# A fourth seven-product slot in the first batch, the tokens' transposes in three calls, and a new hand-made order

## The chip, the cores and the metric

The kernel runs on one core of one Trainium2 chip. The metric is the device time of one execution in microseconds (us); lower is better. Times of the kernel before are given as the median of three runs, with the lowest and the highest.

## The reference

The reference is a gated feed-forward block with a norm ahead of it, for x of 4 batches of 1024 tokens with 512 features, and 2048 hidden features:

```python
scale = cond @ norm_w.T + 1.0
ms = jnp.mean(x * x, axis=-1, keepdims=True)
h = x * (scale[:, None, :] * jax.lax.rsqrt(ms + EPS))
u = h @ up_w.T                       # 512 -> 2 x 2048
val, gate = jnp.split(u, 2, axis=-1)
h = val * jax.nn.gelu(gate, approximate=False)
hq = act_quant(h)                    # 8 bits, one scale per token
wq = weight_quant(down_w)            # -1, 0, 1 times one scale
y = hq @ wq.T                        # 2048 -> 512
return y + x
```

## The kernel before

**Tiling.** The tokens go batch by batch. The hidden features are cut into NJ = 16 blocks of 128, and the kernel counts "slots" g = 0 to 63: block j of batch b. The up-projection is made in fp16 with a high and a low part of both operands, in matmuls of 128x128 by 512 tokens. There are two ways to make one block:

- *plain* (`plain`, line 712; the steps `gate`, `gelu`, `value`, `out`): for each half of the tokens 12 matmuls for the gate and 12 for the value, so 48 for a block. ACT makes the gelu from the gate's bank (L758), DVE the product of value and gelu (L768).
- *seven products* (`product`, line 697; the class `Slot`, whose steps are numbered as `slot.g.n`): Strassen's scheme in Winograd's form, seven products of 6 matmuls, so 42 for a block. The products share the banks A, B and E, each starting from what another left there; ACT copies banks between (L804 `first_copy`, L812 `fourth_copy`, L819 `fifth_copy`), makes two gelus (L826, L843), and DVE makes two sums and two products (L832, L840, L849, L852). It needs the sums of quarters of the weights (`s_sum`, then `s_high`, `s_low` for the fp16 parts, L436, L453, L457), which are also written to DRAM for the later batches (`s_spill`, L469). A block that is made by a slot in the first batch gets these sums transposed at once (`s_turn`, L475), two DMAs for a block.

Batches 1 to 3 are made by slots throughout. In the first batch blocks below FAST = NJ - 3 = 13 are plain, and 13, 14 and 15 are made by slots.

**What else the first batch does.** It loads and scales all up-projection weights (`w_load`, `w_range` on ACT in two halves at L322, `w_factor`, `w_scale`), loads the down-projection weights twice: once for their mean (`d_load`, L515, and `d_sum`) and once for rounding (`d_fetch`, L546, then `d_round` on ACT, L550). It also prepares the second batch's tokens in four groups a = 0 to 3 of 256 tokens: `t_load`, `t_square`, `t_root`, `t_scale`, `t_sum`, then `t_high` (ACT, L665) and `t_low` (DVE, L669) write the fp16 parts into a tile `nx`, and `t_turn` (SP, L672) transposes it with a DMA into R. `t_high` and `t_low` come in three parts: the first 2 of 7 quarters, the third, the last 4. The tile `nx` comes from a pool with a single buffer under its tag, so that group a + 1 can be written only when the transpose of group a is done:

```python
self.nx = wpool.tile(
    [P, C_ALL, 2, HALF], F16, name=f"nx_{self.b}_{self.a}", tag="nx", bufs=1
)
```

`d_load.2` and `d_load.3` overwrite places in R which squares of the first tokens (`first_sum`, ACT, L1128) use as scratch. `d_fetch.0` and `d_fetch.1` take places of the tokens' other tiles.

**The order.** Outside the first batch a planner with costs and due times places the side work. The first batch's order is written out: the string FIRST_BATCH is a list of steps, and `take` issues them one after the other. Each engine works off its own queue in this order and waits at the head of it; a step far down the list runs early if its engine is free and its data are there, and late if a step ahead of it on the same engine waits. All DMAs are issued by SP, in the order of the list.

```python
def take(steps):
    for step in steps.split():
        name, *at = step.split(".")
        STEPS[name](*map(int, at))
```

The steps of a slot are, from 0 on: first, first_copy, fourth, fourth_copy, fifth, fifth_copy, second, second_gelu, third, third_out, gate, gate_sum, gate_gelu, value, value_sum, value_out. Of them PE does 0, 2, 4, 6, 8, 10 and 13.

Of the kernel before, what the change touches and what calls it, by code (L numbers as in the profile page):

```python
# [36 lines left out]
C_ALL = 7  # L37
# [14 lines left out]
def glu_quant_kernel(  # L52
# [10 lines left out]
    PE, ACT, DVE, POOL, SP = nc.tensor, nc.scalar, nc.vector, nc.gpsimd, nc.sync  # L63
# [7 lines left out]
    NJ = FF // P  # L71
# [71 lines left out]
    FAST = NJ - 3  # L143
# [434 lines left out]
    class Tokens:  # L578
# [92 lines left out]
        def turn(self):  # L671
            SP.dma_start_transpose(  # L672
                t_view(self.b)[:, self.a].rearrange("p c l k t -> p (c l k) t"),
                self.nx.rearrange("p c l d -> p (c l d)"),
            )
# [627 lines left out]
    def t0_order(n):  # L1303
# [39 lines left out]
        "t_low": lambda a, n: toks[a].low(DVE, n), "t_turn": lambda a: toks[a].turn(),  # L1343
# [13 lines left out]
    def take(steps):  # L1357
# [8 lines left out]
        x_low.0 d_sum.4 x_low.2 o_whole.1.0.1 x_low.3 gate.0.1 w_scale.2.0 out.1.0 w_scale.2.1 w_factor.3  # L1366
        rows_high.2 s_sum.0.2 value.0.1 s_high.0.0 rows_low.2 rows_turn.2 d_sum.5 s_low.0.0 c_largest
        gelu.0.1 gate.1.1 w_scale.3.0 s_sum.1.0.1 t_square.0.0 s_sum.0.3.1 w_load.9 o_WHOLE.3.2.1 s_high.0.1
        w_scale.3.1 s_sum.1.1.1 rows_high.3 value.1.1 s_low.0.1.1 s_spill.0.0 s_sum.1.2.1 s_sum.1.3.1
        s_high.1.0 d_load.0 rows_low.3 w_load.10 gelu.1.1 rows_turn.3 w_range.4 out.1.1 gate.2.0 out.0.1  # L1370
        d_sum.6 w_factor.4 w_range.5 o_sum.0 value.2.0 w_scale.4.0 o_sum.1 w_scale.4.1 w_factor.5 s_high.1.1
        s_low.1.1 w_scale.5.1 c_over gate.2.1 w_gain.2 w_scale.5.0 c_range rows_high.4 s_low.1.0.1
        s_spill.1.0 s_sum.2.1 gelu.2.0 o_sum.2 rows_high.5 value.2.1 d_load.1 gelu.2.1 o_high.1 s_sum.2.0.1
        out.2.0 d_sum.7 rows_low.4 rows_turn.4 gate.3.0 o_high.3 s_sum.2.2.1 s_sum.2.3.1 d_sum.2 out.2.1
        rows_low.5 value.3.0 w_gain.4 gelu.3.0 o_high.2 o_low.1 w_load.6 s_high.2.0 o_low.3 gate.3.1
        s_spill.2.1 s_high.2.1 d_sum.3 w_load.7 s_low.2.1.1 o_sum.3 w_load.11 d_sum.0 rows_turn.5 o_low.2
        w_range.6 value.3.1 s_low.2.0.1 s_sum.3.0 d_sum.1 w_factor.6 s_sum.3.1 c_spread w_scale.6.0 c_rows
        max.0.0.0 gate.4.0 s_spill.4.1 w_scale.6.1 s_spill.3.1 out.3.0 s_spill.2.2 rows_high.6 s_spill.2.0
        max.1.0.0 o_high.0 value.4.0 s_sum.3.2.1 gelu.3.1 o_low.0 w_range.7 rows_low.6 rows_turn.6 gate.4.1
        s_high.3.0 s_sum.3.3.1 out.3.1 t_square.0.1 w_factor.7 gelu.4.0 t_root.0 s_low.3.0.1 s_high.3.1  # L1380
        value.4.1 w_load.8 gelu.4.1 s_spill.3.0 w_scale.7.1 s_sum.4.0.1 c_copy t_load.1 d_total w_scale.7.0
        s_low.3.1.1 s_sum.4.1.1 rows_high.7 c_undo out.4.0 gate.5.0 w_range.8 out.4.1 s_sum.4.2.1 rows_low.7
        rows_turn.7 value.5.0 s_high.4.0 s_low.4.0 w_factor.8 max.0.1.0 w_scale.8.0 w_gain.6 gelu.5.0
        c_store out.5.0 s_spill.5.1 d_spread w_scale.8.1 gate.5.1 s_spill.3.2 rows_high.8 c_load max.1.0.1
# [3 lines left out]
        t_scale.0.0 s_spill.8.1 t_scale.0.1 out.5.1 t_high.0.1 t_high.0.0 s_low.5.0.1 w_gain.8 gate.6.1
        w_range.10 t_sum.0.0.1 s_spill.5.0 s_sum.6.0 s_spill.4.2 gelu.6.1 t_low.0.0 s_spill.7.1 s_sum.6.2.1
        s_sum.6.1.1 value.6.1 t_sum.0.2.1 w_factor.10 t_sum.0.3 s_high.6.0 t_sum.0.1.1 w_scale.10.1  # L1390
        s_low.6.0.1 s_sum.7.0 w_scale.10.0 rows_low.9 rows_turn.9 gate.7.0 t_high.0.2 w_gain.10 gelu.6.0
        t_low.0.2 rows_high.10 value.7.0 t_low.0.1 t_square.1.1 t_turn.0 s_sum.6.3.1 out.6.0 t_square.1.0
# [10 lines left out]
        rows_high.12 max.3.1.0 s_sum.10.1 w_load.13 t_low.1.2 t_square.2.1 value.9.1 s_spill.9.2 rows_low.12
        rows_turn.12 s_high.10.1 t_square.2.0 s_low.10.1.1 out.9.0 s_high.10.0 gate.10.0 t_low.1.0 gelu.10.0
        s_low.10.0.1 t_low.1.1 t_turn.1 max.3.1.1 value.10.0 s_sum.11.0.1 s_sum.11.1.1 gelu.9.1 w_range.13
        out.9.1 s_sum.11.2.1 s_sum.11.3 gate.10.1 w_factor.13 w_scale.13.0 t_root.2 w_load.14 t_scale.2.0
        t_load.3 gelu.10.1 t_scale.2.1 value.10.1 t_sum.2.1.1 w_gain.12 t_sum.2.0 out.10.0 s_high.11.0
# [386 lines left out]
    c = slice(HALF, D)  # L1794
# [29 lines left out]
```

## Time and profile before

| | |
|---|---|
| median of 3 runs (lowest, highest) | 721.4 us (721.0 to 722.2) |
| profiled execution, its time | 721.38 us |
| profiled execution, span of the trace | 719.6 us |
| granted TensorE clock over the span | 1.0 |
| share of the span busy: PE, DVE, ACT, POOL | 99%, 82%, 59%, 18% |
| matmuls in the trace | 3670 |
| TensorE's share of the chain that ended last | 99% |
| HBM read and written | 52.71 MB and 23.09 MB |

PE is the matmul engine (TensorE), PEld its weight loads, DVE VectorE, ACT ScalarE, POOL GpSimd, SP the engine that issues the DMAs. "L712" is line 712 of the kernel before. In a row of a group, a name such as `nx<-xt` is the tile that is written and the one that is read; "x51" is the number of instructions; behind the bar stand busy time in us and the mean duration of one in ns; behind the next one the idle time of the engine just before them, and who ended it. In a timeline a row begins with the start and the duration in us, and a bracket gives the engine's idle time before it. SPq is SP's DMA queue: the duration there is that of the issue, and the landing comes later.

### The profile page before, as it was taken

What the parts mean: (1) busy time and instruction counts of PE and PEld (TensorE: products, weight loads), DVE (VectorE), ACT (ScalarE), POOL (GpSimd) and SP (SyncE); (2) the same over time, 40 slices, a digit from 0 to 9 for tenths busy, and PEclk for the clock granted to TensorE, in tenths of its full rate; (3) what the DMA queues carried; (4) which work ended last, traced back from release to release, by engine and by line L of the source; (5) the groups of instructions that cost most, each with busy time, mean ns of one, the idle gap of its engine ahead of it and who ended that gap; (6) DMA issues with size and microseconds to landing.
All of it is one profiled execution on the core that took longest, in us unless ns stands there. A gap on an engine that the chain in (4) does not pass through costs nothing.

```text
span 719.6 us, 10204 instructions
## 1 busy us (share of the span) xinstructions
PE 713.8 (99%) x3670; PEld 360.2 (50%) x3670; DVE 591.3 (82%) x888; ACT 422.2 (59%) x700; POOL 128.9 (18%) x133
## 2 busy tenths in 40 slices
PE   8999999999999999999999999999999999999998
PEld 4544444444444446665444445665444444445854
DVE  8899899888698879897788868876689888755896
ACT  6998875776568774544335676544433665333473
POOL 1611323421100115340100031460020000000120
PEclk9999999999999999999999999999999999999999
DMA  7899878999886656777744646775944544453253
GB/s 277 265 279 288 250 192 240 260 213 234 225 188 120 131 161 147 206 179 169 150 101 118 130 96 195 172 172 160 210 103 103 102 102 102 100 103 94 104 155 138
DMA packets 225204, 121.18 MB, mean 168 GB/s; under 512 B 187113, under 2 KB 196733, under 8 KB 225154
## 3 DMA queue, kind: packets, MB, share of 16 engines
q1 hardware_dynamic: 225002, 120.41, 66.8%
q8 instruction: 28, 0.46, 0.3%
q14 instruction: 22, 0.18, 0.1%
q10 hardware_dynamic: 152, 0.13, 0.1%
HBM read 52.71 MB, written 23.09 MB: 105 GB/s over the span
## 4 chain that ended last, share of the span: by engine, by line
PE 99%; ACT 0%; DVE 0%; issue 0%
PE A L697 37%; PE E L697 18%; PE po L1061 9%; PE B L697 9%; PE pg L712 9%; PE pv L712 9%; PE po_end L1013 4%; PE pz L1178 1%; PE ptx L1162 1%; PE pv L783 0%; PE po_B L1061 0%; PE pg L783 0%; PE pw L382 0%; PE po_E L1061 0%; PE po_A L1061 0%; ACT R L1128 0%
## 5 line engine op out<-in xcount | busy, mean ns | idle before, releaser
L697 PEld LDWEIGHTS <-SXY 128*128 128x128 f16 x2058 | 201.3, 98 | 235.6
L697 PE MATMUL A<-R,SXY 128*128 128x512 f16 x1140 | 263.4, 379 | 0.0
L697 PE MATMUL E<-R,SXY 128*128 128x512 f16 x576 | 140.0, 379 | 0.0
L832 DVE SCALAR_TENSOR_TENSOR H<-A,sg,t 128x512 f32<-128x512 f32 x51 | 38.2, 750 | 71.7 <-PE A L697 71.5
L984 DVE TENSOR_TENSOR H<-H,am 128x1024 f32<-128x1024 f32 x64 | 76.0, 1212 | 0.0
L843 ACT ACTIVATE t<-t,sg 128x512 f32<-128x512 f32 x51 | 36.7, 720 | 63.0 <-DVE t L840 62.8
L697 PE MATMUL B<-R,SXY 128*128 128x512 f16 x294 | 71.5, 379 | 0.0
L903 DVE TENSOR_REDUCE gm<-H 128x512 f32<-128x1024 f32 x56 | 69.0, 1233 | 1.1
L712 PEld LDWEIGHTS <-SXY 128*128 128x128 f16 x390 | 38.0, 98 | 46.0 <-DVE SXY L424 0.4
L826 ACT ACTIVATE t<-B,sg 128x512 f32<-128x512 f32 x51 | 35.1, 687 | 38.5 <-PE B L697 38.3
L919 POOL PARTITION_ALL_REDUCE am<-R x8 | 14.4, 1795 | 231.5 <-DVE R L905 231.5
L1061 PE MATMUL po<-wd,R 128*128 128x256 fp8e4 x416 | 52.4, 273 | 0.0
L819 ACT COPY t<-A 128x512 f32<-128x512 f32 x51 | 29.7, 581 | 35.8 <-PE A L697 35.4
L1061 PEld LDWEIGHTS <-R 128*128 128x128 bf16 (+1 forms) x448 | 43.8, 98 | 8.9
L812 ACT COPY v<-E 128x512 f32<-128x512 f32 x51 | 29.9, 586 | 31.2 <-PE E L697 30.8
L804 ACT COPY B<-A 128x512 f32<-128x512 f32 x51 | 29.2, 572 | 32.1 <-PE A L697 31.5
L712 PE MATMUL pg<-R,SXY 128*128 128x512 f16 x204 | 46.8, 379 | 0.0
L852 DVE SCALAR_TENSOR_TENSOR H<-v,sg,t 128x512 f32<-128x512 f32 x51 | 40.0, 785 | 6.6 <-ACT t L843 6.6
L849 DVE TENSOR_TENSOR v<-A,v 128x512 f32<-128x512 f32 x51 | 34.8, 683 | 10.8 <-PE A L697 8.7
L712 PE MATMUL pv<-R,SXY 128*128 128x512 f16 x186 | 43.4, 379 | 0.0
L992 ACT ACTIVATE H<-H 128x1024 f32<-128x1024 f32 x38 | 39.9, 1050 | 5.2 <-DVE H L984 5.2
L905 DVE TENSOR_TENSOR R<-R,gm 128x512 f32<-128x512 f32 x56 | 40.4, 721 | 1.1
(237 smaller groups left out, 944.1 us busy)
## 6 DMA issues: line engine op xcount, KB each, us to landing
SXY<-s_dram SPq DMA_DIRECT2D x46, 256.0 KB, 3.1
H<-in_L_cond_up_w_dram SPq DMA_DIRECT2D x13, 512.0 KB, 4.4
s_dram<-SXY SPq DMA_DIRECT2D x16, 384.0 KB, 3.2
SXY<-s_dram SPq DMA_DIRECT2D x46, 128.0 KB, 3.3
xr<-in_x_dram SPq DMA_DIRECT2D x19, 256.0 KB, 3.0
out_dram<-xr SPq DMA_DIRECT2D x19, 256.0 KB, 2.6
H<-in_x_dram SPq DMA_DIRECT2D x8, 512.0 KB, 6.6
R<-in_L_cond_down_w_dram SPq DMA_DIRECT2D x8, 512.0 KB, 6.5
```

Source lines behind the costliest of these rows:

```text
L697: PE.matmul(o, s[:, w, k, :], operand(g // NJ, c, l, k), start=start and n == 0, stop=stop and n == len(TERMS) - 1, skip_group_check=True,)
L712: PE.matmul(ps, a[k // 2][:, w, k % 2, :], XP[:, l, k, h * TOK : (h + 1) * TOK], start=n == 0, stop=n == len(terms) - 1,)
L826: ACT.activation(self.t1, self.B, AF.Gelu, scale=gain(self.g, 1))
L832: DVE.scalar_tensor_tensor(h_half(self.g, 0), self.A, gain(self.g, 0), self.t1, ALU.mult, ALU.mult)
L843: ACT.activation(self.t2, self.t2, AF.Gelu, scale=gain(self.g, 1))
L849: DVE.tensor_tensor(self.v, self.A, self.v, ALU.add)
L852: DVE.scalar_tensor_tensor(h_half(self.g, 1), self.v, gain(self.g, 0), self.t2, ALU.mult, ALU.mult)
L903: DVE.tensor_reduce(gm[0], v, AX.X, ALU.max, apply_absolute_value=True)
L905: return [largest, lambda: DVE.tensor_tensor(m, m, gm[0], ALU.max)]
L984: DVE.tensor_tensor(v, v, r.to_broadcast([P, 2, TOK]), ALU.mult)
L992: ACT.activation(v, v, AF.Copy, bias=MAGIC)
L1061: PE.matmul(po, w[:, j], m, start=start and j == 0, stop=stop and j == n - 1, skip_group_check=True,)
```

## The change

Three things are changed. Block 12 of the first batch is made by a slot (FAST goes from NJ - 3 to NJ - 4), so blocks 12 to 15 are. `Tokens.turn` takes a part, and transposes the first 2 quarters, the third, or the last 4 (8, 4 and 16 blocks of 128x128) in a DMA of its own; the list calls it three times for each of the four groups. The list itself is new throughout: 619 steps for 601. Lines behind the split are one further down in the kernel after (L697 is L698 there, L672 is L673). Below, the first lines of the list and its end are shown; the middle, left out, is likewise in another order.

```diff
--- before.py
+++ after.py
@@ -140,7 +140,7 @@
     )
     A21 = R[:, 0, 6144 : 6144 + 768].bitcast(F16).rearrange("p (n w f) -> p n w f", n=3, w=2)
 
-    FAST = NJ - 3
+    FAST = NJ - 4
     T0 = wd.bitcast(F16).rearrange("p a b c d -> p (a b c d)")
     T0 = T0.rearrange("p (c l k t) -> p c l k t", c=4, l=2, k=2)
 
@@ -668,10 +668,11 @@
             for n, f in self.parts()[slice(part, None if part is None else part + 1)]:
                 eng.tensor_tensor(n[:, :, 1], f, n[:, :, 0], ALU.subtract)
 
-        def turn(self):
+        def turn(self, part=None):
+            c = slice(0, C_ALL) if part is None else (slice(0, 2), slice(2, 3), slice(3, 7))[part]
             SP.dma_start_transpose(
-                t_view(self.b)[:, self.a].rearrange("p c l k t -> p (c l k) t"),
-                self.nx.rearrange("p c l d -> p (c l d)"),
+                t_view(self.b)[:, self.a, c].rearrange("p c l k t -> p (c l k) t"),
+                self.nx[:, c].rearrange("p c l d -> p (c l d)"),
             )
 
 
@@ -1340,7 +1341,7 @@
         "t_load": token_load, "t_square": lambda a, h: toks[a].square(h),
         "t_root": lambda a: toks[a].root(), "t_scale": lambda a, h: toks[a].scale(made["sc"], h),
         "t_sum": lambda a, n, e=0: toks[a].sum(n, BOTH[e]), "t_high": lambda a, n: toks[a].high(n),
-        "t_low": lambda a, n: toks[a].low(DVE, n), "t_turn": lambda a: toks[a].turn(),
+        "t_low": lambda a, n: toks[a].low(DVE, n), "t_turn": lambda a, n: toks[a].turn(n),
         "max": lm, "o_whole": lambda m, k, h: t0_whole(m, k, h, POOL),
         "o_WHOLE": t0_whole, "o_sum": t0_order,
         "o_high": lambda c: t0_high(T0_AT[c], c), "o_low": lambda c: t0_low(T0_AT[c], c),
@@ the list FIRST_BATCH: first lines, and from the second group of token transposes on
- w_load.3 d_load.6 d_load.3 d_load.4 d_load.5 t_load.0 d_load.2 s_sum.0.1 o_whole.2.2.0 gate.1.0
- x_scale.6 w_range.3 x_scale.7 gelu.1.0 o_whole.0.0.0 turn.4 w_range.2 turn.5 turn.6 turn.7 w_load.5
- x_high.1 value.1.0 w_factor.2 x_high.0 d_load.7 s_sum.0.0.1 w_load.4 x_low.1 x_high.3 x_high.2
...
- gate.11.1 t_high.2.1 t_low.2.0 t_square.3.1 t_low.2.1 t_square.3.0 s_low.12.0.1 t_turn.2 t_root.3
- w_factor.14 value.11.1 s_sum.12.3.1 gelu.11.1 t_scale.3.0 w_scale.14.0 s_sum.13.0.1 w_scale.14.1
- out.11.1 s_high.12.1 s_low.12.1 gate.12.0 gelu.12.0 w_load.15 s_spill.12.0 s_sum.13.2 out.11.0
- s_sum.13.1.1 value.12.0 s_sum.13.3.1 s_high.13.0 rows_high.14 s_low.13.0.1 s_turn.13.0 s_sum.14.0
- s_high.13.1 t_high.3.0 gate.12.1 s_low.13.1.1 s_sum.14.2 w_range.15 s_spill.13.0 s_turn.13.1
- s_sum.14.1.1 rows_low.14 s_spill.13.2 s_sum.14.3.1 value.12.1 rows_turn.14 w_factor.15 gains
- w_scale.15.1 t_scale.3.1 s_high.14.0 s_low.14.0 t_sum.3.0.1 s_turn.14.0 w_scale.15.0 out.12.0
- slot.13.0 t_sum.3.2.1 s_sum.15.0 slot.13.2 slot.13.1 t_sum.3.1.1 max.4.0.0 s_high.14.1 s_low.14.1
- rows_high.15 slot.13.4 s_spill.14.0 w_gain.14 t_high.3.1 t_sum.3.3.1 slot.13.6 slot.13.5 max.4.0.1
- s_turn.14.1 gelu.12.1 s_sum.15.2.1 out.12.1 s_spill.14.2 slot.13.7 s_high.15.0 slot.13.13 d_fetch.0
- t_high.3.2 s_sum.15.3.1 s_sum.15.1.1 slot.14.0 rows_low.15 rows_turn.15 slot.14.1 t_low.3.0
- slot.14.2 t_low.3.2 slot.13.3 slot.14.6 slot.13.14 s_spill.10.2 d_round.0 s_low.15.0.1 slot.13.8
- t_low.3.1 s_turn.15.0 max.5.0.0 s_high.15.1 s_low.15.1 w_gain.15 slot.14.7 slot.14.4 d_fetch.1
- t_turn.3 max.5.0.1 slot.13.10 slot.14.5 max.4.1.0 slot.14.13 slot.13.9 slot.13.11 slot.15.0
- max.4.1.1 slot.13.12 s_turn.15.1 max.5.1.0 slot.15.1 slot.15.2 slot.14.3 slot.14.14 s_spill.15.0
- s_spill.15.2 slot.15.6 slot.15.7 d_fetch.3 max.5.1.1 slot.13.15 slot.14.8 slot.14.9 slot.15.3
- s_spill.11.2 d_round.1 slot.15.4 d_fetch.2 s_spill.14.1 max.6.0.0 s_spill.15.1 slot.15.5 slot.14.10
- s_spill.13.1 s_spill.12.2 d_sign.0 max.6.0.1 slot.15.13 slot.14.11 d_sign.1 max.6.1.0 slot.14.12
- max.6.1.1 slot.15.14 slot.14.15
+ d_load.2 w_load.3 d_load.6 d_load.4 t_load.0 s_sum.0.1 o_whole.0.0.0 gate.1.0 w_range.3 x_scale.7
+ o_whole.2.2.0 x_scale.6 turn.4 w_range.2 gelu.1.0 turn.5 w_load.4 turn.6 turn.7 d_load.5 value.1.0
+ d_load.3 x_high.2 w_factor.3 s_sum.0.0 d_load.7 x_high.0 c_largest w_factor.2 x_high.1 s_sum.0.2.1
+ x_low.0 x_high.3 s_sum.0.3 s_high.0.0 x_low.1 x_low.2 w_scale.2.0 s_low.0.0 w_scale.3.1 x_low.3
...
+ s_low.13.0.1 s_turn.13.0 s_sum.13.3.1 rows_low.14 slot.12.0 slot.12.1 t_low.2.2 slot.12.2
+ rows_turn.14 max.3.1.0 s_high.13.1 s_low.13.1 s_sum.14.0.1 slot.12.4 slot.12.5 slot.12.3 t_low.2.0
+ s_spill.13.0 w_gain.14 s_sum.14.2 s_turn.13.1 slot.12.6 slot.12.7 out.11.1 s_spill.13.2 slot.12.13
+ t_turn.2.2 s_sum.14.3 w_range.15 slot.13.0 s_sum.14.1.1 t_square.3.1 w_factor.15 slot.13.2 slot.13.1
+ max.3.1.1 t_square.3.0 slot.12.14 s_high.14.0 slot.13.6 t_root.3 t_scale.3.1 w_scale.15.1
+ w_scale.15.0 slot.12.8 s_low.14.0.1 s_turn.14.0 rows_high.15 t_sum.3.0 slot.13.4 rows_low.15
+ s_spill.14.0 s_sum.15.0.1 slot.12.10 t_turn.2.0 slot.13.5 t_scale.3.0 t_sum.3.2 slot.13.7 slot.12.9
+ slot.13.3 slot.13.13 rows_turn.15 slot.12.11 s_high.14.1 t_sum.3.3 s_low.14.1.1 slot.12.12 slot.14.0
+ slot.14.1 slot.13.14 s_turn.14.1 s_sum.15.1.1 slot.14.2 s_sum.15.2.1 t_sum.3.1.1 s_spill.14.2
+ s_high.15.0 s_low.15.0 t_low.2.1 max.4.0.0 t_high.3.2 slot.14.6 t_high.3.0 slot.12.15 s_spill.15.0
+ slot.13.8 s_turn.15.0 t_low.3.2 slot.14.3 w_gain.15 slot.14.4 slot.14.5 d_fetch.0 s_sum.15.3.1
+ t_turn.2.1 t_low.3.0 slot.13.10 slot.13.9 d_fetch.1 s_high.15.1 s_low.15.1 s_turn.15.1 slot.14.13
+ slot.13.11 slot.13.12 max.4.0.1 slot.15.0 slot.14.7 slot.14.14 slot.15.1 max.5.0.0 t_turn.3.0
+ slot.15.2 slot.13.15 slot.15.3 s_spill.11.2 slot.15.6 max.5.0.1 t_turn.3.2 max.4.1.0 slot.14.8
+ slot.15.7 d_round.1 s_spill.13.1 max.4.1.1 slot.15.4 d_fetch.2 gains s_spill.15.2 max.5.1.0
+ d_round.0 s_spill.9.2 slot.14.10 slot.15.5 slot.14.9 d_sign.0 max.5.1.1 slot.15.13 slot.14.11
+ t_high.3.1 slot.14.12 slot.15.14 d_sign.1 t_low.3.1 t_turn.3.1 slot.14.15 max.6.0.0 d_fetch.3
+ max.6.0.1 max.6.1.0 s_spill.15.1 s_spill.10.2 s_spill.14.1 max.6.1.1
```

More of the change, by code (lines that the diff above doesn't have):

```diff
@@ L1368, in glu_quant_kernel @@
[L1368 to L1372, printed above, removed]
@@ L1388, in glu_quant_kernel @@
[L1388 to L1392, printed above, removed]
@@ L1403, in glu_quant_kernel @@
[L1403 to L1407, printed above, removed]
@@ new lines, in glu_quant_kernel @@
+        t_high.1.2 s_low.9.1.1 s_sum.10.3 gate.9.1 out.9.0 s_spill.10.1 t_high.1.0 s_spill.9.0 s_high.10.0
+        w_load.13 t_low.1.2 s_low.10.0.1 value.9.1 t_turn.1.2 s_high.10.1 w_scale.12.0 t_high.1.1
+        s_sum.11.1.1 gelu.9.1 s_sum.11.0 rows_high.12 gate.10.0 t_low.1.0 t_turn.1.0 t_square.2.0
+        rows_low.12 t_square.2.1 out.9.1 w_range.13 rows_turn.12 s_sum.11.2.1 value.10.0 t_low.1.1
+        s_low.10.1.1 gelu.10.0 max.3.0.1 s_high.11.0 t_turn.1.1 s_sum.11.3 s_low.11.0.1 w_load.14 gate.10.1
```

72 lines of the change are left out of this document (42 added, 30 removed).

## The prediction

> **What bounds the kernel now.** I read first the busy shares and the chain that ended last (the page's parts 1 and 4), then the busy time by stretches, then the chain in order of time around the end of the first batch.
>
> ```profile
> PE 713.8 (99%) x3670; PEld 360.2 (50%) x3670; DVE 591.3 (82%) x888; ACT 422.2 (59%) x700; POOL 128.9 (18%) x133
> PE 99%; ACT 0%; DVE 0%; issue 0%
> ```
>
> ```profile
> 0.00:20.00 20.00, 17.30 (x86) 9.49 (x87) 16.17 (x77) 13.51 (x31) 4.40 (x9) 1.00 0.74 259
> 100.00:120.00 20.00, 20.00 (x95) 9.06 (x93) 19.64 (x33) 12.50 (x24) 7.29 (x7) 1.00 0.76 249
> 155.00:690.00 535.00, 535.00 (x2811) 274.82 (x2810) 431.36 (x566) 284.32 (x448) 78.31 (x79) 1.00 0.62 144
> ```
>
> In the second block the columns are the stretch, its length, then the busy time of PE, weight loads, DVE, ACT and POOL, the granted clock, the DMA share and GB/s. TensorE (PE) is the bound, and has no gap: 535.00 us busy of 535.00 after the first batch, 20.00 of 20.00 in its middle. Two things follow. A matmul that goes away is worth its pitch. And there is no slack downstream in which lost time could come back: whatever PE waits is added to the end in full. DVE is nearly as full in the first batch (19.64 of 20), so the order in which the queues are served decides whether anything is late.
>
> ```profile
> 150.55 2.59 PE pv L712 x12
> 153.14 1.29 PE A L697 x6
> ```
>
> A matmul costs 2.59/12 = 0.216 us in the plain block and 1.29/6 = 0.216 in the slot, so only their number matters.
>
> **The saving.** Block 12 goes from 48 matmuls (four groups of 12) to 42 (seven products of 6): 6 x 0.216 = 1.3 us less on PE. That is all that the change can gain. ACT gives up two gelus and gets one slot's copies; of the slots' sums that POOL and DVE share, POOL gets 27 in the new list where it had 18, and in the quoted stretch it is busy 7.29 of 20 and can take them. I cost these at nothing: DVE, the fuller of the two, is eased by them. If that cover were gone, one cast or subtraction late would be 0.6 to 1.2 us by the rows of these below.
>
> **The new wait, which carries the forecast.** The fp16 copy of a group of tokens, nx, has one buffer. Group 3 may be written into it (t_high.3.2, t_high.3.0, on ACT) only when all transposes of group 2 have landed. Before, t_turn.2 stood ahead of t_high.3.0 in the list. Now t_turn.2.1, the smallest part of it, is the 14th step behind t_high.3.2, and on SP behind s_spill.15.0, s_turn.15.0 and d_fetch.0. So ACT stops at t_high.3.2 until a transpose has been issued and has landed. Behind it on ACT's queue are t_high.3.0, slot.14.3, w_gain.15 and slot.14.5. The last is the copy of slot 14's fifth product out of bank A; PE's slot.14.13 (the value product) writes this bank, and all of PE is behind it.
>
> When does PE want it? The trace has slot 14's first product, and slot 15's with ACT's copy of it:
>
> ```profile
> 159.45 1.46 PE L697 MATMUL A<-R 128*128 128x512 f16 x6
> 168.51 1.46 PE L697 MATMUL A<-R,SXY 128*128 128x512 f16 x6
> ```
>
> ```profile
> 170.06 0.57 ACT L804 COPY B<-A 128x512 f32<-128x512 f32 x1 [1.07 <-PE A L697]
> ```
>
> With one product less ahead of it, slot 14 starts at 159.45 - 1.30 = 158.15 (in the trace's clock). slot.14.13 is the seventh product from there in the list (14.0, 14.2, 14.6, 13.8, 14.4, 13.10, 14.13), so it is wanted at 158.15 + 6 x 1.295 = 165.9.
>
> When does t_turn.2.1 land? It starts from slot 14's first copy, slot.14.1: in the trace such a copy starts 170.06 - 168.51 = 1.55 after its product, here 159.7. Then come s_high.15.0 on ACT, s_low.15.0 on POOL, and four issues on SP:
>
> ```profile
> L453 ACT CAST s_rows<-H 128x512 f16<-128x512 f32 x6 | 3.7, 610 | 0.0
> ```
>
> ```profile
> 155.65 1.16 POOL L457 TENSOR_TENSOR s_rows<-H,s_rows 128x512 f16<-128x512 f32 x1 [1.01 <-ACT s_rows L453]
> ```
>
> ```profile
> 138.69 4.29 SPq L672 DMA_TRANSPOSE R<-nx  x1
> 158.13 0.57 SPq L469 DMA_DIRECT2D s_dram<-s_rows  x1
> 158.75 0.43 SPq L546 DMA_DIRECT2D dn<-in_L_cond_down_w_dram  x1
> 163.55 1.24 SPq L475 DMA_TRANSPOSE SXY<-s_rows  x1
> 284.80 1.19 SPq L483 DMA_TRANSPOSE SXY<-s_dram  x1
> ```
>
> Copy done 160.3, s_high to 160.9, s_low to 162.1; s_spill.15.0 (0.57) from 162.2, s_turn.15.0 (1.24) from 162.8, d_fetch.0 (0.43) from 164.1, t_turn.2.1 from about 164.7 (gaps of some 0.05 between issues are in these rows). The trace has no 4-block transpose of nx: the nearest are those of the later batches, the last row above being one of 4 blocks, and the load just ahead of it in the queue.
>
> ```profile
> DMA to landing us min/median/max: 2.7/3.9/5.3
> dn<-in_L_cond_down_w_dram SPq DMA_DIRECT2D x3, 512.0 KB, 4.7
> ```
>
> The first row is for the line of those transposes (4 and 12 blocks), the second for the loads of d_fetch between 155 and 180. Alone, a 4-block one should be near 2.7 to 3.2. But d_fetch.0, issued 0.6 before, needs 4.7, until 164.1 + 4.7 = 168.8, on the same queue. I take the load as the nearer row and put the transpose just behind it: landed at 169.2 (bounds 167.9 and 169.7).
>
> Then ACT works off what stands before PE's need:
>
> ```profile
> L665 ACT CAST nx<-xt 128x1024 f16<-128x1024 f32 x6 | 6.3, 1042 | 0.1
> L360 ACT ACTIVATE sg<-sw,dx 128x4 f32<-128x4 f32 x7 | 2.0, 292 | 0.0
> L819 ACT COPY t<-A 128x512 f32<-128x512 f32 x51 | 29.7, 581 | 35.8 <-PE A L697 35.4
> L812 ACT COPY v<-E 128x512 f32<-128x512 f32 x51 | 29.9, 586 | 31.2 <-PE E L697 30.8
> 147.75 0.62 ACT L665 CAST nx<-xa 128x512 f16<-128x512 f32 x1
> ```
>
> 1.04 + 0.62 + 0.59 + 0.29 + 0.58 = 3.1, or 2.8 since neighbours overlap by about 0.1. PE goes on at 169.2 + 2.9 = 172.1, where 165.9 was wanted: **6.2 us lost** (4.9 with the early landing, 6.9 with the late one). What was late behind it, DVE's t_low.3.2 and the remaining products of slots 13 and 14, moves with PE and adds nothing.
>
> In the old trace t_turn.2 was issued at 138.69 and t_high.3.0 ran at 147.75 without a wait, so this is a wait that did not exist.
>
> **PE's rate after standing still.** Nothing in this trace shows PE after an idle stretch in the middle. The nearest rows are at its start:
>
> ```profile
> 3.66 2.31 PE L1178 MATMUL pz<-H 128*128 128x512 f16 x5
> 9.22 0.59 PE L1178 MATMUL pz<-H 128*128 128x512 f16 x2
> ```
>
> Five matmuls take 2.31 (0.43 to 0.46 each), later two take 0.59 (0.22 from one to the next, the rest being the last one's own length); the granted clock reads 1.00 over both. PE thus began at half rate and was at full rate by 9.2. A stop of 6 us may bring the half rate back. It costs nothing if not; at worst the half of some 6 us, 3.0. I take 1.7, a little over the middle. The Trainium skill, "TensorE: Matmul & The Clock Gate", section "What's actually happening", says that PE drops to half clock after an idle window of about 3.4 us and comes back after about 3.4 us of work; by that rule the loss would be half of 3.4, 1.7 us. The start agrees with its two rates; that an idle stretch in the middle brings it back, no row here shows.
>
> **The start.** The new list begins with d_load.2, then w_load.3; before, w_load.3 came first and d_load.2 six steps later.
>
> ```profile
> 7.97 0.38 SPq L306 DMA_DIRECT2D H<-in_L_cond_up_w_dram  x1
> 8.61 10.73 SPq L515 DMA_DIRECT2D R<-in_L_cond_down_w_dram  x4
> SPq L515 <- ACT R L1128: 8.1, 1, 8.1
> 15.42 0.66 ACT L1128 ACTIVATE R<-H 128x512 f32<-128x512 f32 x1
> R<-in_L_cond_down_w_dram SPq DMA_DIRECT2D x8, 512.0 KB, 6.5
> H<-in_L_cond_up_w_dram SPq DMA_DIRECT2D x13, 512.0 KB, 4.4
> 21.65 0.74 ACT L1155 ACTIVATE H<-H,rs 128x512 f32<-128x512 f32 x1
> 22.26 0.64 ACT L322 ACTIVATE H<-H 128x512 f16<-128x512 f32 x1
> 23.55 1.91 PE L1162 MATMUL ptx<-ident,H 128*128 128x128 f32 x16
> ```
>
> The 8.1 us wait is d_load.3's, for the last of three squares of ACT's (L1128) whose scratch it overwrites; d_load.2 overwrites the scratch of the first of them (15.42 to about 16.1). So w_load.3, issued at 7.97 before, now waits behind d_load.2 until about 16.6, and lands 4.4 to 6.5 later, 21.0 to 23.1, in a stretch where the queue is full: I take 23.0. Its range (w_range.3, twice 0.61) now stands ahead of x_scale.6 on ACT, which then ends at about 23.0 + 1.2 + 0.7 = 25.0. PE's transposes turn.6 need it, the third of four groups of four, at 23.55 + 8 x 0.11 = 24.4. **0.6 us lost** (0 to 1.5).
>
> **Three calls for one.** The 28 blocks took 4.29 us of SP; three calls of 8, 4 and 16 take about 4.1 by the 4- and 8-block rows. Slot 12 adds two transposes of its rows (s_turn.12, 1.24 each), issued while slots 13 to 15 are still being made. Neither is what ends last. At the end d_fetch.3 stands behind t_turn.3.1, and its rounding on ACT ahead of work that slot 17 needs: it comes out within 0.1 us of the need. I add **0.1** (0 to 1.5).
>
> **The sum.** -1.3 + 0.6 + 6.2 + 0.1 + 1.7 = +7.3 on the profiled execution's 721.38 us (span 719.6), which is the median of the runs shown (721.4): **728.7 us**.
>
> **Rivals.**
> - *The stop without a change of rate.* For it: the granted clock is 1.00 in every row quoted. Against: the start's two rates. 721.4 + 5.6 = 727.0; with the early landing and no early stall 721.4 - 1.3 + 4.9 = 725.0.
> - *The saving alone, no slower.* If t_turn.2.1 is out early enough, ACT never stops: the six matmuls go, 720.1, within what counts as the same. It decides at a landing of 165.9 - 2.9 = 163.0 or earlier, that is, an issue by 160 instead of 164.7, so s_low.15.0 and s_spill.15.0 would have to run five microseconds earlier than slot.14.1 lets them. Against it stands that ACT serves its queue in order. That the plan's places on one queue differ from how they run is all that speaks for it.
> - *Small stalls only.* The main stop is mostly hidden (t_turn.2.1 landing near 164), the early one counts: 720.7 to 722.5.
> - *More congestion.* Early and late stalls at their upper ends with the half rate: 721.4 - 1.3 + 1.5 + 6.9 + 0.3 + 2.4 = 731.2.
>
> **How the numbers follow.** The stop with half rate (728 to 730): 0.50. The stop at full rate (725.0 to 727.9): 0.31. Congestion (over 730): 0.10. Small stalls: 0.04. Saving alone: 0.05. The range 724.9 to 731.0 holds the first two and most of the third, and leaves out the small ones. A difference of 0.2% (1.44 us) is about what a measurement of this kernel can tell from none; the saving alone is 0.18%, so it would be faster by more only with a further gain of 0.2 us: faster 0.02, same 0.06, slower 0.92.
>
> **What would show it.** In the changed kernel's profile: 6 matmuls fewer in all; ACT's cast nx<-xt of 128x1024 idle for some 6 us ahead of it, released by a DMA on nx, at about 163 to 169; PE idle from about 166 to 172, ended by ACT's copy t<-A; then matmuls at 0.43 us for some microseconds, or at 0.216 (the first rival). At the start PE idle before its transposes at about 24, ended by ACT's scaling. If PE is 100% busy from 155 to 690 and the span is 718.3, the step that t_turn.2.1 is late was wrong; if PE's gap at 24 is missing, that of w_load.3.

## The result, and the profile after

The changed kernel takes 729.0 us (median of 4 runs, 728.4 to 729.7), the kernel before 721.2 (4 runs): ratio 1.0106, 95% interval 1.0088 to 1.0123, so 7.8 us slower by the medians. The profiled execution took 728.52 us, its span is 726.4. Each group of kernels below was timed beside the kernel before on the same chip, where that took 721.6 to 722.0 us, so the ratios are compared rather than the times. Each trace is one execution, and its time can differ from the median by 2 us.

The page, parts 1 and 4; then PE's waits (engine and line, what it waited for, us in total, times, longest); then the busy time by stretches, with the columns of the prediction:

```profile
PE 714.6 (98%) x3664; PEld 360.1 (50%) x3664; DVE 589.7 (81%) x880; ACT 423.0 (58%) x703; POOL 135.7 (19%) x143
PE 96%; ACT 1%; DMA 1%; DVE 1%; issue 0%; SPq 0%; POOL 0%; ACTq 0%
```

```profile
PE A L698 <- ACT t L820: 5.8, 1, 5.8
```

```profile
165.00:175.00 10.00, 4.18 (x14) 1.60 (x13) 4.02 (x6) 4.20 (x8) 1.15 (x1) 0.68 0.51 127
155.00:690.00 535.00, 529.18 (x2754) 269.64 (x2752) 427.53 (x561) 281.60 (x441) 78.00 (x81) 0.99 0.61 144
```

PE has six matmuls fewer and one gap: 529.18 us busy of 535 where it was 535 of 535. The chain now leaves PE once, to ACT, a DMA and what stood ahead of it. In the ten microseconds around it PE, DVE and ACT are each busy for only about four (4.18, 4.02, 4.20), since each queue is served in order and all of them wait for one late transfer; the granted clock is 0.68 in this stretch.

The place itself, in the timelines of SP's queue, ACT and PE, and in the chain:

```profile
162.91 1.30 SPq L475 DMA_TRANSPOSE SXY<-s_rows  x1
164.30 0.53 SPq L546 DMA_DIRECT2D dn<-in_L_cond_down_w_dram  x1
164.88 1.20 SPq L673 DMA_TRANSPOSE R<-nx  x1
```

```profile
160.64 0.62 ACT L453 CAST s_rows<-H 128x512 f16<-128x512 f32 x1
169.55 1.04 ACT L665 CAST nx<-xt 128x1024 f16<-128x1024 f32 x1 [8.29 <-DMA R<-nx]
171.70 0.57 ACT L820 COPY t<-A 128x512 f32<-128x512 f32 x1
```

```profile
165.04 1.46 PE L698 MATMUL E<-R,SXY 128*128 128x512 f16 x6
172.32 2.72 PE L698 MATMUL A<-wd,R 128*128 128x512 f16 x6 [5.82 <-ACT t L820]
174.84 1.75 PE L698 MATMUL A<-R,SXY 128*128 128x512 f16 x6
176.42 1.46 PE L698 MATMUL E<-wd,SXY 128*128 128x512 f16 x6
```

```profile
164.88 4.49 DMA R<-nx
172.32 4.26 PE A L698 x12
697.15 25.95 PE po_end L1014 x136
```

Read from the top: t_turn.2.1 is issued at 164.88 behind s_turn.15.0 and d_fetch.0 and lands 4.49 later; ACT, idle for 8.29 us, then casts (t_high.3.2) and comes at 171.70 to the copy slot.14.5; PE has stood for 5.82 us, and its next six matmuls take 2.72 where six took 1.46.

What the stop costs is read from start to start. A matmul's bar is 0.38 us long, but the next one starts 0.216 after it, so the idle time in the row is 0.16 short of what is lost. The group at 165.04 would have been followed at 166.34; the next one came at 172.32, 5.98 us later. The twelve matmuls from there to 176.42 take 4.10 us instead of 2.59, 1.51 more. (The chain's 4.26 for them holds the last one's bar as well.)

The granted clock, in half-microsecond stretches at the edges of the half rate:

```profile
168.50:169.00 0.50, 0.00 (x0) 0.00 (x0) 0.00 (x0) 0.00 (x0) 0.00 (x0) 0.58 0.26 51
175.00:175.50 0.50, 0.50 (x3) 0.15 (x1) 0.36 (x1) 0.38 (x1) 0.00 (x0) 0.59 0.42 97
```

It is 1.00 ahead of the first and behind the second of them, and 0.50 in between. So it falls at 168.6, 2.1 us after PE's last bar ends at 166.50, and is back at 175.4: half rate holds for 6.8 us, and PE works in the last 3.1 of them.

The start, in PE's timeline of the kernel before (first two rows) and after, and SP and ACT after:

```profile
6.03 1.54 PE L1178 MATMUL pz<-H 128*128 128x512 f16 x4
20.93 2.79 PE L712 MATMUL pg<-R,SXY 128*128 128x512 f16 x12
```

```profile
6.03 1.86 PE L1179 MATMUL pz<-H 128*128 128x512 f16 x4
21.34 2.79 PE L713 MATMUL pg<-R,SXY 128*128 128x512 f16 x12
23.97 1.91 PE L1163 MATMUL ptx<-ident,H 128*128 128x128 f32 x16
```

```profile
16.98 0.43 SPq L306 DMA_DIRECT2D H<-in_L_cond_up_w_dram  x1
22.06 0.64 ACT L322 ACTIVATE H<-H 128x512 f16<-128x512 f32 x1
23.29 0.73 ACT L1156 ACTIVATE H<-H,rs 128x512 f32<-128x512 f32 x1
```

There is no gap before the 16 transposes at 23.97. But the first plain group comes 0.41 us later than before, mainly because four matmuls at the kernel's start took 1.86 instead of 1.54: PE came out of its half rate later. (At the start of the kernel matmuls run at half rate while the granted clock reads 1.00, so only their lengths show it.) This is an execution's chance and not the change: with the same steps up to there, the first plain group starts at 20.91 in the reordered list below, and anywhere from 20.36 to 24.44 in the traces of the others.

The end, in the chain of the kernel before:

```profile
690.54 25.95 PE po_end L1013 x136
```

PE's last group starts 697.15 - 690.54 = 6.61 us later. The parts make it up: -1.29 (six matmuls) + 5.98 (the stop) + 1.51 (the half rate) + 0.41 (the start) = 6.61.

### The profile page after: what moved, and what is told of

Read it like the earlier page. It is cut to its first block, busy times and chain, and to the rows that moved or that the text cites. A ratio compares the mean times of both kernels' runs of the same rounds, so it can differ in the third digit from the quotient of the medians.

```text
span 726.4 us, 10223 instructions
## 1 busy us (share of the span) xinstructions
PE 714.6 (98%) x3664; PEld 360.1 (50%) x3664; DVE 589.7 (81%) x880; ACT 423.0 (58%) x703; POOL 135.7 (19%) x143
## 4 chain that ended last, share of the span: by engine, by line
PE 96%; ACT 1%; DMA 1%; DVE 1%; issue 0%; SPq 0%; POOL 0%; ACTq 0%
PE A L698 36%; PE E L698 18%; PE po L1062 9%; PE B L698 9%; PE pg L713 8%; PE pv L713 8%; PE po_end L1014 4%; PE pz L1179 1%; DMA R<-nx 1%; PE ptx L1163 1%; DMA R<-s_rows 0%; PE pv L784 0%; PE po_B L1062 0%; PE pg L784 0%; PE pw L382 0%
## 5 line engine op out<-in xcount | busy, mean ns | idle before, releaser
L698 PEld LDWEIGHTS <-SXY 128*128 128x128 f16 x2100 | 205.6, 98 | 241.0 <-issue 0.8
L698 PE MATMUL A<-R,SXY 128*128 128x512 f16 x1146 | 265.1, 379 | 0.0
L698 PE MATMUL E<-R,SXY 128*128 128x512 f16 x582 | 141.4, 379 | 0.0
L698 PE MATMUL B<-R,SXY 128*128 128x512 f16 x300 | 72.9, 379 | 0.0
L820 ACT COPY t<-A 128x512 f32<-128x512 f32 x52 | 30.2, 580 | 37.9 <-PE A L698 37.5
L813 ACT COPY v<-E 128x512 f32<-128x512 f32 x52 | 30.4, 585 | 31.8 <-PE E L698 31.4
L853 DVE SCALAR_TENSOR_TENSOR H<-v,sg,t 128x512 f32<-128x512 f32 x52 | 41.0, 789 | 7.1 <-ACT t L844 7.1
L713 PE MATMUL pg<-R,SXY 128*128 128x512 f16 x180 | 41.3, 379 | 0.0
L997 ACT ACTIVATE R<-H 128x1024 bf16<-128x1024 f32 x38 | 40.1, 1056 | 1.0
```

Of the source, the lines that this page charges most:

```text
L698: PE.matmul(o, s[:, w, k, :], operand(g // NJ, c, l, k), start=start and n == 0, stop=stop and n == len(TERMS) - 1, skip_group_check=True,)
L713: PE.matmul(ps, a[k // 2][:, w, k % 2, :], XP[:, l, k, h * TOK : (h + 1) * TOK], start=n == 0, stop=n == len(terms) - 1,)
L853: DVE.scalar_tensor_tensor(h_half(self.g, 1), self.v, gain(self.g, 0), self.t2, ALU.mult, ALU.mult)
L997: ACT.activation(q, by_tile(v), AF.Copy, bias=-MAGIC)
```

## The experiments

My theory: ACT's stop for the landing of t_turn.2.1 and the half rate after it are the whole loss. Rivals: the slot or the split costs time by itself; the wait only moves; the half rate comes after any stop.

**The list reordered at that place.** Nothing but the places of six steps (the expectation says ten):

```diff
- t_low.2.1 max.4.0.0 t_high.3.2 slot.14.6 t_high.3.0 slot.12.15 s_spill.15.0 slot.13.8 s_turn.15.0
- t_low.3.2 slot.14.3 w_gain.15 slot.14.4 slot.14.5 d_fetch.0 s_sum.15.3.1 t_turn.2.1 t_low.3.0
- slot.13.10 slot.13.9 d_fetch.1 s_high.15.1 s_low.15.1 s_turn.15.1 slot.14.13 slot.13.11 slot.13.12
+ t_low.2.1 max.4.0.0 slot.14.6 slot.12.15 t_turn.2.1 s_spill.15.0 slot.13.8 s_turn.15.0
+ slot.14.3 w_gain.15 slot.14.4 slot.14.5 d_fetch.0 s_sum.15.3.1 slot.13.10 slot.13.9 slot.13.11
+ t_high.3.2 t_high.3.0 t_low.3.2 t_low.3.0 d_fetch.1 s_high.15.1 s_low.15.1 s_turn.15.1 slot.14.13 slot.13.12
```

> The changed kernel with ten steps of its list moved and nothing else: t_turn.2.1 ahead of s_spill.15.0 on SP; t_high.3.2, t_high.3.0 and the two t_low of group 3 behind slot.14.5, slot.13.9 and slot.13.11. Theory (ACT stops for the landing of t_turn.2.1, PE stands behind it, and then runs at half rate for a while): all three go, no gap in PE between 155 and 690, and the six matmuls are gained: 721.2 - 1.3 = 719.9 us, 719.5 to 720.8. Rival 1 (the slot for block 12 or the three transposes cost time by themselves, in queues or in DMA): it stays at 724 or above, with PE gaps elsewhere. Rival 2 (only the place of the wait moves: group 3's transposes are now late for slot 16): a gap of 1 to 3 us before slot 16's first product at about 176, 721 to 723 us.

Measured: 723.26 us, ratio 1.0013 (1.0000 to 1.0027). PE, then ACT, DVE and the chain in its trace:

```profile
20.91 2.79 PE L713 MATMUL pg<-R,SXY 128*128 128x512 f16 x12
158.14 1.46 PE L698 MATMUL A<-R 128*128 128x512 f16 x6
176.36 1.46 PE L698 MATMUL A<-wd,SXY 128*128 128x512 f16 x6 [1.22 <-ACT t L820]
```

```profile
172.59 0.58 ACT L813 COPY v<-E 128x512 f32<-128x512 f32 x1 [3.26 <-PE A L698]
173.65 2.19 ACT L550 ACTIVATE dn<-dn,wsc 128x1024 f32<-128x1024 f32 x2
175.73 0.58 ACT L820 COPY t<-A 128x512 f32<-128x512 f32 x1
```

```profile
171.76 0.73 DVE L853 SCALAR_TENSOR_TENSOR H<-v,sg,t 128x512 f32<-128x512 f32 x1
```

```profile
691.27 25.95 PE po_end L1014 x136
```

The 5.8 us and the half rate are gone. Slot 14 starts 158.14 - 20.91 = 137.23 us after the first plain group, where the kernel before has 159.45 - 20.93 = 138.52: the six matmuls are worth 1.29 us, measured in place. But they are not gained at the end. A new wait of 1.22 us stands at 176: the copy slot.15.5 (L820) is behind two d_rounds, and these behind the copy slot.15.3 (L813), which waits 3.26 us. The row names PE, but PE had long made that bank; what ends just then, at 172.5, is DVE's slot.13.15 (L853), which gives the tile v back. From the first plain group to the last one 0.75 us are lost and not 1.29 gained (691.27 - 20.91 against 690.54 - 20.93). The trace accounts for it: PE's three waits after 20 us, 1.22, 0.18 and 0.16 us in the rows and 0.16 more each from start to start, are 2.04 us, and -1.29 + 2.04 = 0.75. In the changed kernel these waits do not appear: with PE seven microseconds late, ACT had time for it. The theory is right on the stop. The forecast time was missed, and the second rival has the place and the size of what comes after, but not its cause: PE waits for ACT's copy and not for group 3's transposes.

**The same with block 12 plain** (its slot steps replaced by gate, gelu, value and out at the same places, FAST = NJ - 3). Block 12's values are not the reference's here; the kernel stands for its time alone.

> As the reordered list, but block 12 is made plain (four groups of 12 matmuls at the places where its products stood, and its two s_turn left out). Theory (a matmul that goes away is worth its pitch, nothing else hangs on slot 12): six matmuls of 0.2158 us more than the reordered list, 1.3 us slower than it, so 721.2 us like the kernel before. Rival (the slot eases or loads other queues too): another difference than 1.3 us, with gaps in PE between 140 and 160.

Measured: 727.24 us, ratio 1.0064 (1.0046 to 1.0082), 4 us above the reordered list and not 1.3. PE waits for copies in slots 13 to 17 (3.8 us in all): a list made for a slot does not fit a plain block. The expectation of 1.3 us fails. The rival's other difference came, with PE's gaps at 160 to 195 instead of 140 to 160. From the first plain group to the last, the two traces differ by 4.9 us: six matmuls more are 1.29 of it, the longer waits the other 3.6. This fits the 1.29 us of the slot read above; the rest is what the list does.

**The late transpose moved step by step**, each time t_turn.2.1 alone: ahead of d_fetch.0, ahead of s_turn.15.0, ahead of s_spill.15.0.

```diff
- s_spill.15.0 ... s_turn.15.0 ... d_fetch.0 s_sum.15.3.1 t_turn.2.1
+ s_spill.15.0 ... s_turn.15.0 ... t_turn.2.1 d_fetch.0 s_sum.15.3.1        (first)
+ s_spill.15.0 ... t_turn.2.1 s_turn.15.0 ... d_fetch.0 s_sum.15.3.1        (second)
+ t_turn.2.1 s_spill.15.0 ... s_turn.15.0 ... d_fetch.0 s_sum.15.3.1        (third)
```

> The changed kernel with one step moved: t_turn.2.1 ahead of d_fetch.0 on SP, so issued about 0.6 us earlier and without a 512 KB load just ahead of it. Theory with the load as the reason for the long landing (4.5 us): it lands 3.0 to 3.3 after its issue at 164.3, PE goes on at about 170.3 and stands 3.8 us instead of 5.8. If half rate needs about 3.4 us of standing still, it may or may not come: 724.6 (without) to 726.6 us (with 1.7). Rival (a transpose of nx takes 4.5 us anyway): PE stands 5.2 us, 728 us with half rate.

> The changed kernel with one step moved: t_turn.2.1 between s_spill.15.0 and s_turn.15.0. It fills the series of stops: 5.8 us (half rate after), 3.3 (half rate after) and 1.0 (no half rate). Issued at about 162.9, landed 2.5 to 3.0 later at 165.6, PE goes on at 168.6 and stands 2.0 to 2.4 us. Theory (half rate comes back when a fixed window of about 3.4 us was idle, wholly or for most part): full rate after it, no matmul above 0.22 us. Rival (a share of a shorter window decides): half rate again.

> The changed kernel with one step moved further: t_turn.2.1 ahead of s_spill.15.0, so issued at about 161.6, as soon as t_low.2.1 is done; ACT's order stays. Theory: landed at about 164.8, ACT's t_high.3.2 follows, PE goes on at 167.6 and stands about 1.1 us, at full rate after: 721.2 - 1.3 + 1.1 = 721.0 us (720.4 to 722). Rival (half rate comes back after any stop): 1.7 us more, 722.7, with matmuls of slot 14 at 0.43 us.

Measured: 726.36 us (ratio 1.0050, 1.0032 to 1.0068), 724.67 (1.0035, 1.0020 to 1.0050) and 722.71 (1.0006, 0.9989 to 1.0023). The chain of the first, and PE's timeline of the first, second and third:

```profile
165.41 2.52 DMA R<-nx
170.88 4.44 PE A L698 x12
```

```profile
170.88 2.66 PE L698 MATMUL A<-wd,R 128*128 128x512 f16 x6 [3.27 <-ACT t L820]
```

```profile
171.41 1.46 PE L698 MATMUL A<-wd,R 128*128 128x512 f16 x6 [1.80 <-ACT t L820]
```

```profile
169.10 1.46 PE L698 MATMUL A<-wd,R 128*128 128x512 f16 x6 [1.03 <-ACT t L820]
```

Two things follow. The transpose of 4 blocks lands 2.52 us after its issue when no load is just ahead of it, and 4.49 with d_fetch.0's 512 KB ahead: two of the six microseconds came from that neighbour. And the stop becomes shorter step by step (5.8, 3.3, 1.8, 1.0 us, each of the last three a little under what was expected), with half rate after the two long ones (six matmuls in 2.72 and 2.66) and not after the short ones (1.46). The rival, half rate after any stop, falls by these matmuls.

The times alone would not decide it. The third was put at 0.2 us below the kernel before (the rival at 1.5 above) and is 0.7 above it; its trace has other waits of 0.96, 0.83, 0.17 and 0.60 us. The second's traced execution took 726.92 us, 2.3 more than its median: its first plain group starts at 24.44, 3.5 us later than in the kernel before, since PE's half rate at the start of the kernel held longer there (its first 16 transposes take 3.62 us instead of 2.14). In the first the granted clock fell at 171.0, 3.4 us after PE's last bar had ended and 0.1 after PE had started again, and was back at 174.4. It came close to no half rate at all: five of its six executions have a granted clock of 0.997 or 0.998 over the span, and the fastest (724.75 us) has 1.000.

**Three repairs, and two of them.** To the reordered list: slot.13.15 ahead of max.4.0.1 and d_round.0 ahead of slot.15.3 (two repairs); and d_load.1 ahead of w_load.9 and w_load.11 (three).

```diff
- w_load.9 ... w_load.7 w_range.6 s_spill.3.1 w_load.11 d_load.1
+ w_load.7 d_load.1 w_load.9 w_load.11 w_range.6 s_spill.3.1
```

> The reordered list with two more repairs. On ACT, d_round.0 goes ahead of slot.15.3, and on DVE slot.13.15 ahead of max.4.0.1, since in the reordered list's trace PE waits 1.2 us at 176.4 for a copy (L820) that stands behind two d_rounds, which in turn stand behind a copy that DVE's late slot.13.15 holds up for 3.3 us. On SP, d_load.1 goes ahead of w_load.9 and w_load.11, since two traces show PE waiting 0.8 us at 76 for the mean of the down weights. Theory: every wait that the new list adds is gone, what remains is the six matmuls: 1.3 us below the kernel before of the same chip (ratio 0.9982, 0.997 to 0.9995). Rival (ACT has too much to do after slot 14, whatever the order): a wait of 0.5 to 1.5 us comes back at slots 16 or 17, ratio 0.9995 to 1.001.

> As the kernel with three repairs, but the loads for the mean stay in the new list's order (d_load.1 behind w_load.9 and w_load.11). Theory: PE waits at 70 to 77 us in some executions (0.8 to 2 us, as loads land early or late) and not in others: a median 0.4 to 1.0 us above that of three repairs, and a wider spread. Rival (these waits are only a profile's): no difference.

Measured: 724.23 us (ratio 1.0043, 1.0026 to 1.0059) and 723.65 (1.0025, 1.0016 to 1.0033). Neither beats the reordered list, and the median with three repairs is the higher one, against the expectation. But three of its nine executions (726.7 to 727.1 us) show a granted clock of 0.997 or 0.998, which points to a longer stop with half rate that no trace here has; the median of the other six is 723.2. Whether the repair of the load order helps stays open. The wait for L820 is gone, others of 0.5 to 0.8 us at slots 16 and 17 are there instead. What suggested the load order were two traces with waits in the middle of the batch; here SP and PE in one of them (t_turn.2.1 ahead of s_spill.15.0), and SP in the reordered list, where PE waits for nothing there:

```profile
49.50 4.69 SPq L406 DMA_TRANSPOSE SXY<-H  x1
54.92 3.93 SPq L406 DMA_TRANSPOSE R<-H  x1
62.27 0.58 SPq L515 DMA_DIRECT2D R<-in_L_cond_down_w_dram  x1
```

```profile
70.51 2.75 PE L713 MATMUL pg<-R 128*128 128x512 f16 x12 [0.96 <-ACT g L759]
76.68 0.38 PE L528 MATMUL pmean<-wpart,one 128*128 128x1 f32 x2 [0.83 <-DVE wpart L523]
```

```profile
49.32 3.50 SPq L406 DMA_TRANSPOSE SXY<-H  x1
54.38 2.27 SPq L406 DMA_TRANSPOSE R<-H  x1
59.83 0.78 SPq L515 DMA_DIRECT2D R<-in_L_cond_down_w_dram  x1
```

The two lists are the same there. The issue of a transpose takes 4.69 and 3.93 us in the execution with waits, 3.50 and 2.27 in the other, and everything behind it on SP comes later. So single waits of up to 1 us at 70 to 93 come and go with the execution; that the long issues are their cause is read from one pair of traces.

**One call for groups 0 to 2**, on the list with three repairs, at the place of each group's last part.

> The three repairs, with the transposes of token groups 0, 1 and 2 in one call each again, at the place of each group's last part (group 3 stays in three). Theory (the split takes the early parts out of the way, and only a small transpose is left at the end): group 2's one call of 28 blocks is issued at 161.2, takes 4.3 us of SP and lands 5.8 to 7.4 later, at 167.0 to 168.6 instead of 164; ACT's casts of group 3 wait, and behind them copies of slots 14 and 15; s_spill.15.0 and s_turn.15.0 are issued 3 us later, and slot 15's fourth product needs them at 168.5: PE stands 1 to 3 us: 1 to 3 us slower than three repairs. Rival (the split is worth nothing): within 0.5 us of it.

Measured: 729.22 us, ratio 1.0113 (1.0093 to 1.0133), 5 us above three repairs. SP's and ACT's timeline:

```profile
164.87 4.46 SPq L673 DMA_TRANSPOSE R<-nx  x1
171.24 1.04 ACT L665 CAST nx<-xt 128x1024 f16<-128x1024 f32 x1 [1.79 <-DMA R<-nx]
```

The one call holds SP for 4.46 us and ACT waits for its landing, then slot 15 waits for its rows. By its trace, 2.7 us of PE's waits between 173 and 197 are more than with three repairs; 2.3 us stand at 77 to 95, where waits come and go as shown above, and 0.7 at the start. So the split is worth some 3 us in this list, and the rival (nothing) falls. The 5 us lie above the expected 1 to 3; what is beyond the 2.7 is not separated.

**All late places repaired, with the mean's loads early and late.** Steps at the end moved: the maxima behind the sums that PE waits for, d_sign.1 into an idle place, and t_high.3.1, t_low.3.1, t_turn.3.1 right behind the other parts. The first kernel also has d_load.1 right behind d_load.0 and d_sum.0, d_sum.1 ahead of gelu.3.1.

> The reordered list with all late places moved. At the end of the first batch: the maxima (max.4.0.1, max.5.1.0, max.5.1.1) behind the sums that PE's products wait for, d_round.0 and d_sign.1 into ACT's idle places, and the last part of group 3 (t_high.3.1, t_low.3.1, t_turn.3.1) right behind its other parts. In the middle: d_load.1 right behind d_load.0, and d_sum.0 and d_sum.1 ahead of gelu.3.1, where ACT stood idle for 2.2 us. Theory (every wait of PE that the new list adds is known, and slot 12 is worth its six matmuls): PE waits for nothing after 20 us, and the ratio to the kernel before is 0.9982 (0.997 to 0.9995). Rival (other waits come and go with the DMA queues, in some executions, that no profile of ours has caught): no gap in the profile, but a ratio of 1.000 or above and a spread of several us.

> As the kernel with all repairs, but d_load.1, d_sum.0 and d_sum.1 stay where the new list has them. Theory (the mean of the down weights, needed by PE at 76, is ready at 74 to 77 depending on how long SP's transposes take to issue): 0.3 to 1.5 us above the kernel with all repairs in the median, with a wider spread, and in some profiles waits at 70 to 93. Rival: no difference.

Measured: 723.17 us (ratio 1.0017, 1.0008 to 1.0026) and 721.58 (0.9999, 0.9991 to 1.0008). The opposite of the expectation: with the sums late it is 1.6 us better. In the traces, first with the sums early, then late:

```profile
60.25 0.63 ACT L322 ACTIVATE H<-H 128x512 f16<-128x512 f32 x1 [2.41 <-DMA H<-in_L_cond_up_w_dram]
71.76 2.75 PE L713 MATMUL pg<-R 128*128 128x512 f16 x12 [1.20 <-ACT g L759]
```

```profile
185.58 1.46 PE L698 MATMUL A<-R 128*128 128x512 f16 x6 [1.03 <-ACT t L820]
```

With the sums early ACT's gelu is late for PE at 71. ACT was not full: it had stood 2.41 us at 60 for a load of up-projection weights, 0.67 in the other trace. That load is issued behind SP's transposes, which took 5.12 us to issue with d_load.1 put ahead of them and 3.76 without. So the traces point at the early load on SP rather than at the sums on ACT; as both were moved at once, and an issue of 4.69 us came without d_load.1 too (above), this is not shown.

**The last version:** the better one of these, with d_fetch.2 ahead of t_turn.3.1 and d_spread behind gate.5.1.

> The kernel of the last study with the mean's loads and sums left in the new list's order (721.6 us against 721.9 before), with two steps moved: d_fetch.2 ahead of t_turn.3.1 on SP, since in that kernel's trace PE waits 1.0 us at 185.6 for a copy (L820) behind a d_round that waits for d_fetch.2; and d_spread behind gate.5.1 on PE, so that the matmul for the mean, which waited 0.2 to 0.9 us in several traces, is asked for 2.6 us later. Theory: no wait of PE after 20 us is left in the profile, and the six matmuls come through: ratio 0.9982 (0.997 to 0.9993), about 720.6 where the kernel before has 721.9. Rival (there is always another transfer that comes late in some executions): ratio 0.9993 to 1.0005, with a gap of 0.3 to 1 us elsewhere.

Measured: 721.67 us, ratio 0.9999 (0.9990 to 1.0008). PE's two listed waits after 20 us are

```profile
91.84 2.75 PE L713 MATMUL pg<-R,SXY 128*128 128x512 f16 x12 [0.24 <-ACT g L759]
188.49 1.46 PE L698 MATMUL E<-R,SXY 128*128 128x512 f16 x6 [0.38 <-DVE t L841]
```

The rival was right, with smaller gaps than it named. The version is level with the kernel before and does not beat it: from the first plain group to the last its trace is 0.2 us longer than the trace of the kernel before (691.14 - 21.30 against 690.54 - 20.93). The two rows cost 0.40 and 0.55 us from start to start, and delays too short to be listed (0.25 at 86, 0.11 at 185 and some below) make it about 1.5 us, a little more than the six matmuls give.

**The load at the start**, on the list with all repairs: w_load.3 behind d_load.6, d_load.4 and t_load.0.

> As the kernel with all repairs, but w_load.3 goes behind d_load.6, d_load.4 and t_load.0 on SP, 1.6 us later than the new list has it. This tests the step of the prediction on the start: w_load.3 (issued at 16.98 behind d_load.2) was there by 22.06, and x_scale.6 was done 0.8 us ahead of turn.6. Theory (the mechanism is right and the landing was put too late): it lands at about 24.5 to 25.5, x_scale.6 ends at 26.5 to 27.4, and PE waits 1.6 to 2.6 us at about 25 for ACT. Rival (ACT has slack or the queue does not matter there): no gap at 25.

Measured: 729.41 us, ratio 1.0105 (1.0087 to 1.0124). ACT, PE and the stretches:

```profile
27.84 0.63 ACT L322 ACTIVATE H<-H 128x512 f16<-128x512 f32 x1 [5.83 <-DMA H<-in_L_cond_up_w_dram]
29.84 1.97 PE L1163 MATMUL ptx<-ident,H 128*128 128x128 f32 x8 [5.01 <-ACT H L1156]
30.00:35.00 5.00, 5.00 (x17) 2.79 (x18) 2.65 (x7) 3.73 (x7) 0.88 (x2) 0.51 0.53 217
```

The chain w_load.3, w_range.3, x_scale.6, turn.6 decides at once when the load is late, as the prediction had it. Behind three more transfers the load landed at about 27.8 instead of the expected 24.5 to 25.5, PE waited 5.0 us and not 1.6 to 2.6, and the half rate followed (granted clock 0.51 in the stretch after; it fell at 28.1, 3.2 us after PE's last bar, and was back at 34.9). In the changed kernel it is 0.8 us early: x_scale.6 ends at 24.02, turn.6 is due at 23.97 + 8 x 0.11 = 24.85.

## Why the prediction was right, by its steps

- **The saving**, 1.3 us: right, 1.29 in place. That the slot costs the other engines nothing was right too, but not because ACT gives up two gelus: the slot makes two of its own, so ACT only gains three copies (700 to 703 instructions).
- **The new wait**, 6.2 us: 5.98 from start to start. The issue was put at 164.7 and came at 164.88, the landing at 169.2 and came at 169.4, with the load just ahead as the reason, which the first shift of t_turn.2.1 bears out (2.52 instead of 4.49 us). ACT's work after it was put at 2.9 and took 172.32 - 169.55 = 2.8.
- **The half rate**, 1.7 us: 1.51. That it comes back is the mechanism and was right; the value was chosen between 0 and 3.0 with no row for it, so its closeness is partly luck. After the 3.3 us stop the twelve matmuls cost 1.7 more than at full rate (170.88 to 175.16 in that trace, 4.28 instead of 2.59). By the Trainium skill, "TensorE: Matmul & The Clock Gate", section "What's actually happening", half rate comes after an idle window of about 3.4 us, and full rate after about 3.4 us of work. The traces agree only roughly. The clock fell 2.1, 3.4 and 3.2 us after PE's last bar (stops of 5.8, 3.3 and 5.0 us), so 3.4 us of standing still are not always needed; stops of 1.0 and 1.8 us left it alone. Full rate was back 3.1, 3.5 and 5.1 us after PE had started again.
- **The start**, 0.6 us: the step that failed. The landing of w_load.3 was put at 23.0, at the late end of 21.0 to 23.1; it was there by 22.06, and PE did not wait. The mechanism was right and its margin of 0.8 us is thin.
- **Three calls for one**: they were put at about 4.1 us of SP and took 2.54, 1.29 and 1.20 for group 2, so 5.0; nothing but t_turn.2.1's landing held PE.
- **d_fetch.3**, 0.1 us: no wait is seen.
- The prediction's total of +7.3 against +7.1 in the profiled execution (+7.8 by the medians) owes part of its closeness to chance: the 0.6 that did not come was nearly replaced by 0.41 of PE's own late start.
- **The rival of the saving alone** (720.1 us) was weighed as if the rest of the list were sound. It is not: when the stop is taken away, other waits of the new list come out, and after four rounds of repair it is level with the kernel before (0.9999). In the traces the account closes: waits of 0.1 to 1.2 us at changing places take what the six matmuls give. Whether one of them is always there, and so whether an order exists that gains the 1.3 us, stays open.

## What to carry to other kernels

Where queues are written by hand, look for a tile with a single buffer: the step that writes it again must stand behind the issue of the last reader on the other queue, or the writer's whole engine waits for a landing. Put no large load just ahead of the small transfer that somebody waits for. And when one big stop is found, do not book the rest of the list as sound: the stop gives all other engines time, and what it hid comes out when it goes. Read what a stop costs from the starts of the matmuls around it, and not from the idle time alone.

## What the runs showed of the hardware

- A stop of PE has a second price. After stops of 3.3, 5.0 and 5.8 us PE ran at half rate for the next 3 to 5 us, at 1.5 us more for twelve matmuls after 5.8 (4.10 for 2.59 us) and 1.7 after 3.3; after 1.8 us and less it did not. Each length is from one trace.
- In these three traces the granted clock was at half for 3.4, 6.8 and 6.8 us, and it fell 3.4, 3.2 and 2.1 us after PE's last matmul. Whether two stops of the same length cost the same was not measured.
- The same 4-block transpose lands after 2.52 us with no load just ahead of it (2.42 in the second shift) and after 4.49 us behind a 512 KB load on its queue.
- SP's time to issue the same transpose differs between executions (3.50 and 4.69 us, 2.27 and 3.93), and everything behind it on SP comes later.
- How long PE's half rate holds at the kernel's start differs too: with the same steps, the first plain group starts at 20.36 to 24.44 us.
